# Groups of tokens side by side through the layers with a lag, and softmax scores made a second time in transposed form

## The chip, the cores and the metric

The kernel runs on one core of one Trainium2 chip. The metric is the device time of one execution in microseconds (us). A core has TensorE (PE), which multiplies matrices and writes the results to PSUM; VectorE (DVE), ScalarE (ACT) and GpSimd (POOL), which work element by element and in reductions; and SyncE (SP), which here only issues DMAs. Each engine takes its instructions from its own queue in order; they meet through semaphores. In the profile PE's matmuls and its loads of weights (PEld) have rows of their own. One float32 matmul of the program leaves two records, one transpose on PE leaves one.

## The reference

The input x is 8 sequences of 256 tokens with 128 features, in float32. Eight residual steps follow each other, each on a layer norm of x:

```
x += causal softmax attention (one head, key width 64, values through two matrices)
x += LN(t + relu(t w1 + b1) w2 + b2) * gamma + beta,   t = LN(x)      (FFN, expert 0 alone counts)
x += linear attention: (theta phi^T / sqrt(128)) g                     (no softmax)
x += the same FFN
x += retention: 16 heads, key width 8, value width 16, decaying causal mask, head norm, silu gate
x += silu(t wg) * (t wu) wd                                            (weights are int32 / 127)
x += softmax attention: 16 heads of width 8, no mask, output matrix
x += the same silu FFN
```

In the seventh step, for every head, the output row of a query is sum over keys of exp(s - m) v / sum over keys of exp(s - m), where s is the score of the query with the key and m may be any number that is the same for all keys of the query; the row's maximum keeps the exponentials in range.

## The kernel before

The 2048 tokens are cut into four groups of 512 (two sequences each). A group's x lives in SBUF as a tile of 128 partitions by 4 by 128. Every layer is a Python generator for one group: it records instructions up to a `yield`, and a driver at the end of `hybrid` decides which generator records next. A scheduling layer below takes the recorded instructions in that order as priorities, gives each tile a buffer of its pool, and may bring forward an instruction whose inputs are ready earlier; what comes out is one fixed order on each engine.

**The driver.** `parts()` lists layer by layer, and in a layer group by group. Two parts are active at a time, with the condition that they belong to different groups, and they record a step in turn. So two groups of the same layer (or the last of one layer and the first of the next) share the engines. A part that says `HEADS_NEXT` (retention and softmax attention, after their projections) waits until it is the older one of the two; its heads are copied and its values made beside the older part's heads.

**PSUM** has eight banks of 128 x 512 floats. Before: two buffers of two banks (`two_banks`), two of one bank (`one_bank`), two `held_bank`.

**Layer norm** (`layernorm`) takes statistics on DVE, the inverse root as a power on POOL, and four scalings on DVE. `transposed` turns the result on PE (L237) and copies it on ACT (L239). The first FFN (`ffn_relu`) has two layer norms, and POOL adds in between; its matmuls are L361 and L375.

**Heads.** A head has only 8 features, which would be 8 rows of the PE array. `spread_heads` (L386) copies the 16 heads' queries and keys by 16 DMAs on SP's queue (L391) so that head h lies at partitions 32 (h mod 4) to 32 (h mod 4) + 7; matmuls of heads in different groups of 32 rows may then stand in the array at once. The tile `spread` has two buffers.

**Retention** (`retention`) computes scores of 64-token chunks (L470, tiles of 8 rows by 64 columns), a state between chunks (L495, L514) and chunk values (L522, 64 by 64 tiles with 17 moving columns), and then a head norm on DVE.

**Softmax attention** (`softmax_attention`) works on pairs of heads, 16 pairs a group (2 sequences by 8). For a pair:

- `probabilities`: four score matmuls (L642; queries in rows, keys in columns) into two banks, the maxima of the rows on DVE (L648, 128 x 1024 in one instruction), and four exponentials on ACT (L654, 128 x 256 each), because each 128 queries of a head need the bias of their own maxima.
- `turned`: eight transposes of 128 x 128 on PE (L667) into held banks, and two copies of 128 x 512 on DVE (L671), so that keys lie on the partitions.
- `weighted` with `weighted_values` (L401): four matmuls with values of 32 columns a head (8 values, then ones, which give the sum of the exponentials).

After four pairs `by_query` (L406) copies the bank, turns it on PE (L414), and `divided` divides by the sums. After eight, `finished` applies the output matrix. The three steps of a pair are recorded one iteration apart: scores of pair n, transposes of pair n-1, values of pair n-2.

## Time and profile before

| | |
|---|---|
| time, median of 3 runs | 775.63 us (773.04 to 775.73) |
| the profiled execution's own time | 774.3 us |
| its span from first to last instruction | 772.2 us |
| mean granted TensorE clock | 0.829 of full |
| PE matmul busy | 653.3 us (85% of the span) |
| DVE busy | 436.2 us (56%) |
| ACT busy | 215.7 us (28%) |
| POOL busy | 108.1 us (14%) |
| table loads on ACT | 16, 1.283 us each |
| copies of heads on SP's queue | 128, 32 KB each, 0.624 us each at the median |

The stages lie one after the other: loads to 20 us, causal attention 20 to 72, first FFN 72 to 130, linear attention 130 to 156, second FFN 156 to 215, retention from 215 to about 440 with the silu FFN between 426 and 486, softmax attention 486 to 750 with the last FFN between its groups, and the end to 772.

How to read it: busy time is the time in which at least one instruction of the engine ran, so that matmuls that run side by side count once, and their mean duration says little about their pace. The pace is the distance from the start of one run of instructions to the start of the next. PEclk is the granted share of TensorE's clock. A row of a group gives its busy time and the mean length of one instruction, and then the idle time just ahead of it and what ended that.

### The profile page before, as it was taken

Reading aid. Unit: us, or ns where it says so; the run is one execution under the profiler, and the core shown is the slowest. Engines: PE = TensorE matmul, PEld = TensorE weight load, DVE = VectorE, ACT = ScalarE, POOL = GpSimd, SP = SyncE. Lnnn points to the kernel's source line nnn. Section 1 sums busy time; section 2 is a strip of 40 time slices with the busy share of each in tenths; the row PEclk is TensorE's granted clock in tenths of the full one; section 3 lists DMA queues with packets and bytes.
Section 4 is the critical chain, followed back from the end, with each engine's and each line's share of the span. In section 5 each row is a group of like instructions: output and inputs, shape, how many; then the busy total and the mean of one; then the engine's idle time right before and its main releaser. Section 6 shows DMA issues by size and latency. Waiting matters only on the chain.

```text
span 772.2 us, 12437 instructions
## 1 busy us (share of the span) xinstructions
PE 653.3 (85%) x5038; PEld 421.3 (55%) x5038; DVE 436.2 (56%) x1120; ACT 215.7 (28%) x468; POOL 108.1 (14%) x107
## 2 busy tenths in 40 slices
PE   0989574984588979989889978999999999999985
PEld 0556443662433865655556655666666666565653
DVE  3662546645583445434533455588688688766542
ACT  0333120221010011100100222544454454456541
POOL 5021233324251010110110022100000000000000
PEclk9875867995876556757655899899999999999997
DMA  7000000000003000010010000210010010000000
GB/s 227 4 1 0 1 0 1 1 0 0 1 10 45 3 1 2 12 18 2 12 18 2 2 0 1 40 16 1 1 28 2 1 28 1 1 14 1 15 14 14
DMA packets 10232, 10.49 MB, mean 14 GB/s; under 512 B 1776, under 2 KB 8512, under 8 KB 10176
## 3 DMA queue, kind: packets, MB, share of 16 engines
q1 hardware_dynamic: 9024, 9.11, 5.9%
q10 hardware_dynamic: 1152, 0.59, 0.4%
q8 instruction: 40, 0.66, 0.3%
q14 instruction: 16, 0.13, 0.1%
HBM read 4.45 MB, written 1.05 MB: 7 GB/s over the span
## 4 chain that ended last, share of the span: by engine, by line
PE 72%; DVE 15%; POOL 5%; ACT 3%; DMA 2%; issue 2%; POOLq 0%; ACTq 0%; SPq 0%; DVEq 0%
PE ps_two L642 9%; PE ps_one L401 8%; PE ps_held L667 8%; PE ps_held L522 5%; PE ps_two L361 4%; PE ps_one L495 4%; PE ps_two L470 3%; DVE ln_y L209 3%; POOL ln_rstd L217 3%; PE ps_one L607 2%; PE ps_one L237 2%; PE ps_two L598 2%; PE ps_two L437 2%; PE ps_two L599 2%; PE ps_one L375 2%; PE ps_one L567 2%
## 5 line engine op out<-in xcount | busy, mean ns | idle before, releaser
L654 ACT ACTIVATE l_p<-ps_two,l_nmax 128x256 f32<-128x256 f32 x256 | 100.5, 475 | 108.1 <-DVE l_nmax L648 108.1
L648 DVE TENSOR_REDUCE l_nmax<-ps_two 128x4 f32<-128x1024 f32 x64 | 78.3, 1223 | 41.1 <-PE ps_two L642 40.1
L217 POOL TENSOR_TENSOR ln_rstd<-ln_rstd,mhalf 128x4 f32<-128x4 f32 x40 | 40.6, 1016 | 415.8 <-DVE ln_rstd L216 415.8
L237 PE MATMUL ps_one<-ident,ln_y 128*128 128x128 f32 x128 | 31.3, 377 | 71.6 <-DVE ln_mv L205 42.3
L671 DVE COPY l_pT<-ps_held 128x512 f32<-128x512 f32 x128 | 82.6, 676 | 9.3 <-PE ps_held L667 9.2
L642 PE MATMUL ps_two<-spread 8*128 8x256 f32 x512 | 79.4, 404 | 0.3 <-DMA spread<-qk 0.3
L667 PE MATMUL ps_held<-ident,l_p 128*128 128x128 f32 x512 | 74.6, 282 | 0.8 <-ACT l_p L654 0.8
L401 PE MATMUL ps_one<-l_pT,values 128*32 128x256 f32 x512 | 73.3, 385 | 0.0
L667 PEld LDWEIGHTS ps_held<-ident,l_p 128*128 128x128 f32 x512 | 56.9, 142 | 24.0 <-ACT l_p L654 13.6
L237 PEld LDWEIGHTS ps_one<-ident,ln_y 128*128 128x128 f32 x128 | 19.9, 176 | 84.3 <-issue 54.7
L642 PEld LDWEIGHTS ps_two<-spread 8*128 8x128 f32 x512 | 48.3, 185 | 26.8 <-issue 20.3
L239 ACT COPY yT<-ps_one 128x512 f32<-128x512 f32 x32 | 18.8, 587 | 137.5 <-PE ps_one L237 137.3
L209 DVE TENSOR_SCALAR ln_y<-x,ln_mv,ln_rstd 128x128 f32<-128x128 f32 x128 | 45.2, 398 | 20.7 <-POOL ln_rstd L217 20.6
L522 PEld LDWEIGHTS ps_held<-values,r_s 64*64 64x64 f32 x1024 | 46.4, 188 | 6.0 <-issue 5.2
L522 PE MATMUL ps_held<-values,r_s 64*64 64x17 f32 x1024 | 48.0, 243 | 0.0
L252 DVE TENSOR_TENSOR x<-ps_one,x 128x256 f32<-128x256 f32 (+1 forms) x28 | 15.0, 536 | 48.2 <-PE ps_one L567 21.5
L470 PEld LDWEIGHTS ps_two<-spread 8*64 8x64 f32 x1024 | 27.9, 187 | 26.3 <-issue 19.1
L401 PEld LDWEIGHTS ps_one<-l_pT,values 128*32 128x32 f32 x512 | 27.4, 109 | 26.3 <-issue 12.7
L470 PE MATMUL ps_two<-spread 8*64 8x64 f32 x1024 | 35.6, 290 | 5.0 <-DVE r_s L475 5.0
L495 PE MATMUL ps_one<-values,r_k 64*128 64x272 f32 (+1 forms) x64 | 33.2, 640 | 4.0 <-ACT r_k L488 4.0
L204 DVE BATCH_NORM_STATS2 ln_stats<-x 128x6 f32<-128x128 f32 x128 | 31.7, 272 | 7.9 <-DMA x<-in_x 7.6
L361 PE MATMUL ps_two<-yT,c_f_w 128*128 128x512 f32 x64 | 34.4, 690 | 0.0
(144 smaller groups left out, 893.9 us busy)
## 6 DMA issues: line engine op xcount, KB each, us to landing
spread<-qk SPq DMA_DIRECT2D x128, 32.0 KB
x<-in_x SPq DMA_DIRECT2D x4, 256.0 KB
out<-x SPq DMA_DIRECT2D x4, 256.0 KB
c_f_w<-in_f_w SPq DMA_DIRECT2D x2, 256.0 KB
c_r_tab<-in_r_tab SPq DMA_DIRECT2D x1, 512.0 KB
c_r_vgb<-in_r_vgb ACTq DMA_DIRECT2D x1, 256.0 KB
c_r_qk<-in_r_qk SPq DMA_DIRECT2D x1, 256.0 KB
c_r_vg<-in_r_vg SPq DMA_DIRECT2D x1, 256.0 KB
```

What stands on the lines that cost most here:

```text
L209: nc.vector.tensor_scalar(y[:, i, :], src[:, i, :], mv[:, i, 0:1], rstd[:, i : i + 1], ALU.subtract, ALU.mult)
L237: nc.tensor.transpose(ps[:, i * P : (i + 1) * P], y[:, i, :], ident)
L361: nc.tensor.matmul(ps[:, k, :], w1[:, c * P : (c + 1) * P], yT, start=True, stop=True)
L401: nc.tensor.matmul(o[32 * i : 32 * (i + 1), (j % 2 + 1) * S - weights.shape[1] : (j % 2 + 1) * S], v, weights, start=(n == 0), stop=(n == ...
L470: nc.tensor.matmul(ps[64 * e : 64 * e + 64, k, 64 * jt : 64 * jt + 64], heads[rows, jt // 2, 1, at : at + 64], heads[rows, jt // 2, 0, at ...
L495: nc.tensor.matmul(ps[:, : HEADS * VONE], k[:rows, m, :], v[:rows, 2 * b + m, :, :VONE], start=(c == 0), stop=(c == len(pieces) - 1),)
L522: nc.tensor.matmul(ps[half, VONE * h : VONE * (h + 1)], s[half, h % 4, h // 4 * 2 + m, :], v[half, 2 * b + m, h, :VONE], start=alone, stop ...
L642: nc.tensor.matmul(ps[:, k, m * S : (m + 1) * S], qk[rows, j, 0, at + m * P : at + (m + 1) * P], qk[rows, j, 1, at : at + S], start=True, ...
L648: nc.vector.tensor_reduce(nmax, ps.rearrange("p k (m s) -> p (k m) s", m=2), AX.X, ALU.max, negate=True)
L654: nc.scalar.activation(p[:, k, m * S : (m + 1) * S], ps[:, k, m * S : (m + 1) * S], AF.Exp, bias=nmax[:, 2 * k + m : 2 * k + m + 1],)
L667: nc.tensor.transpose(ps[:, c * S + m * P : c * S + (m + 1) * P], p[:, k, m * S + c * P : m * S + (c + 1) * P], ident,)
L671: nc.vector.tensor_copy(flat(pT[:, 2 * k : 2 * k + 2, :]), ps)
```

## The change

**The driver** gives every group its own clock. Each layer has a length and a number of steps in a table; group g starts at 14 times g; at each turn the group whose clock is lowest records one step and its clock goes forward by the layer's length over its steps. So up to four groups are in different layers at once. Only one group at a time may be in retention, and only one in softmax attention; the next waits at the door.

**Buffers.** There is one spread tile for retention (`spreads[0]`) and one for softmax (`spreads[1]`), both constant tiles that POOL fills at the start: the query half with zeros, the key half with ones (four memsets of 128 x 2048). Likewise `values32[0]` belongs to retention and `values32[1]` to softmax. `one_bank` has three buffers and `held_bank` one. The hidden tile `hT` has three buffers, `probs` four, the gate of retention one; some tiles share a tag to make room. The int32 weights are made float32 in place, and `centre_values`, `prepare_ffn_int` and `prepare_lora` are recorded when group 0 comes to linear attention.

**Softmax attention.** The first scores (`scores`, L641 of the changed kernel) serve the maxima alone. The negated maxima of four pairs are gathered in one tile, turned on PE (L656), copied (L658), and four small DMAs on SP (L661) write them as a ninth row beside each head's queries; the keys have a one in that row. Six iterations later `weights` makes the scores again with keys in rows and queries in columns (L673), over 32 rows of which the ninth subtracts the maximum; the exponential (L681) then needs no bias and takes 128 x 512 at once, and its result has the keys on the partitions, as the values matmul (L691) wants. The transposes and their copies are gone. First scores of pair n and second scores of pair (n-6) with its neighbour exchanged are recorded in turn, two matmuls at a time, so that the four stand in four different row groups. The values of two pairs are recorded together, for four heads in four column groups.

```diff
-        return psum.tile([P, N], F32, tag="one", name="ps_one")
+        return psum.tile([P, N], F32, tag="one", name="ps_one", bufs=3)
-        return psum.tile([P, N], F32, tag="held", name="ps_held")
+        return psum.tile([P, N], F32, tag="held", name="ps_held", bufs=1)
...
+    spreads = []
+    for g in range(2):
+        spreads.append(const.tile([P, 4, 2, N], F32, tag=f"spread{g}", name=f"spread{g}"))
+        nc.gpsimd.memset(spreads[g][:, :, 0, :], 0.0)
+        nc.gpsimd.memset(spreads[g][:, :, 1, :], 1.0)
...
-        heads = spread_heads(qk)
-        v = values32[g % 2]
+        heads = spread_heads(qk, spreads[0])
+        v = values32[0]
...
-        qk = spread_heads(qk)
-        v = values32[g % 2]
+        qk = spread_heads(qk, spreads[1])
+        v = values32[1]
...
-        yield HEADS_NEXT
-
-        def probabilities(b, h2):
...
-            for k in range(2):
-                for m in range(2):
-                    nc.scalar.activation(
-                        p[:, k, m * S : (m + 1) * S], ps[:, k, m * S : (m + 1) * S], AF.Exp,
-                        bias=nmax[:, 2 * k + m : 2 * k + m + 1],
-                    )
+        yield
+        def place(h):
+            return slice(32 * (h % 4), 32 * (h % 4) + KDIM), h // 4
+        def scores(b, h2):
+            ps = two_banks()
+            for m in range(2):
+                for k in range(2):
+                    rows, j = place(2 * h2 + k)
+                    nc.tensor.matmul(
+                        ps[:, k, m * S : (m + 1) * S],
+                        qk[rows, j, 0, b * S + m * P : b * S + (m + 1) * P],
+                        qk[rows, j, 1, b * S : (b + 1) * S], start=True, stop=True,
+                    )
+                yield
+            h = 2 * h2 % 8
+            nc.vector.tensor_reduce(
+                nmax[b, h2 // 4][:, :, h : h + 2].rearrange("p m h -> p h m"),
+                ps.rearrange("p k (m s) -> p k m s", m=2), AX.X, ALU.max, negate=True,
+            )
+        def beside_queries(b, half):
+            ps = one_bank()
+            nc.tensor.transpose(ps[:16, :P], flat(nmax.pop((b, half))), ident)
+            rows = small.tile([16, P], F32, tag="l_rows", name="l_rows")
+            nc.vector.tensor_copy(rows, ps[:16, :P])
+            for m in range(2):
+                for j in range(2):
+                    nc.sync.dma_start(
+                        qk[KDIM : P : 32, 2 * half + j, 0, b * S + m * P : b * S + (m + 1) * P],
+                        rows[8 * m + 4 * j : 8 * m + 4 * j + 4, :],
+                    )
+        def weights(b, h2):
+            ps = [one_bank() for _ in range(2)]
+            for c in range(2):
+                for k in range(2):
+                    rows, j = place(2 * h2 + k)
+                    rows = slice(rows.start, rows.start + 32)
+                    nc.tensor.matmul(
+                        ps[k][:, c * S : (c + 1) * S],
+                        qk[rows, j, 1, b * S + c * P : b * S + (c + 1) * P],
+                        qk[rows, j, 0, b * S : (b + 1) * S], start=True, stop=True,
+                    )
+                yield
+            p = work3.tile([P, 2, N], F32, tag="probs", name="l_p", bufs=4)
+            for k in range(2):
+                nc.scalar.activation(p[:, k, :], ps[k], AF.Exp)
             return p
-        def turned(p):
...
+        def weighted(b, pairs, o):
+            for c in range(2):
+                for k in range(2):
+                    for h2, p in pairs:
+                        h = 2 * h2 + k
+                        i, j = h % 4, h // 4
+                        nc.tensor.matmul(
+                            o[32 * i : 32 * (i + 1), (j % 2) * S : (j % 2 + 1) * S],
+                            v[:, 2 * b + c, h, :], p[:, k, c * S : (c + 1) * S],
+                            start=(c == 0), stop=(c == 1),
+                        )
...
+        LAG = 6
+        nmax, made, ends = {}, [], []
+        for n in range(len(PAIRS) + LAG + 2):
+            first, second = None, None
+            if n < len(PAIRS):
+                b, h2 = PAIRS[n]
+                if h2 % 4 == 0:
+                    nmax[b, h2 // 4] = small.tile([P, 2, 8], F32, tag="l_nmax", name="l_nmax")
+                first = scores(b, h2)
+            if 0 <= n - LAG < len(PAIRS):
+                second = weights(*PAIRS[(n - LAG) ^ 1])
...
-    todo = parts()
-    upcoming = next(todo, None)
-    active = {}
-    while upcoming or active:
-        while upcoming and len(active) < 2 and upcoming[0] not in active:
...
+    layers = (
+        (causal_attention, 8.0, 12),
+        (ffn_relu, 8.0, 5),
+        (prepare, 4.0, 5),
+        (ffn_relu, 8.0, 5),
+        (retention, 20.0, 14),
+        (lambda g: ffn_silu(g, *made["ffn"]), 9.0, 5),
+        (lambda g: softmax_attention(g, made["lora"]), 28.0, 28),
+        (lambda g: last(g, *made["ffn"]), 9.0, 5),
+    )
+    LAG = 14.0
+    at = [LAG * g for g in range(GROUPS)]
+    where = [-1] * GROUPS
+    steps = [None] * GROUPS
+    while any(n < len(layers) for n in where):
+        for g in sorted(range(GROUPS), key=lambda g: at[g]):
+            if where[g] == len(layers):
+                continue
+            if steps[g] is None:
+                n = where[g] + 1
+                among_heads = n in (4, 6)
+                if n == len(layers):
+                    where[g] = n
+                    continue
+                if among_heads and any(where[o] == n and steps[o] for o in range(g)):
+                    at[g] = max(at[g], max(at[o] for o in range(g) if where[o] == n)) + 0.1
+                    continue
+                where[g], steps[g] = n, layers[n][0](g)
+            try:
+                next(steps[g])
+            except StopIteration:
+                steps[g] = None
+            at[g] += layers[where[g]][1] / layers[where[g]][2]
+            break
```

## The prediction

> **What bounds the kernel now.** I read the page's engine totals and forty slices first, then the busy time of each engine by stage, then the costliest groups, then the timeline inside softmax and inside retention, and last the waits of the DMA queue.

> ```profile
> PE 653.3 (85%) x5038; PEld 421.3 (55%) x5038; DVE 436.2 (56%) x1120; ACT 215.7 (28%) x468; POOL 108.1 (14%) x107
> PE   0989574984588979989889978999999999999985
> PEclk9875867995876556757655899899999999999997
> ```

> PE is the busiest engine, but not evenly: the first half has holes, and where retention runs (slices 13 to 22) the granted clock is low. By stage (span, then PE busy, ..., granted clock in the third column from the end):

> ```profile
> 20.00:72.00 52.00, 47.51 (x176) 29.96 (x176) 29.49 (x96) 18.43 (x52) 4.52 (x4) 0.73 0.00 1
> 72.00:130.00 58.00, 35.74 (x176) 23.89 (x174) 29.55 (x111) 7.84 (x12) 18.88 (x17) 0.79 0.00 1
> 130.00:156.00 26.00, 22.37 (x126) 14.90 (x127) 18.29 (x72) 6.39 (x13) 8.78 (x9) 0.88 0.00 1
> 156.00:215.00 59.00, 35.67 (x182) 24.05 (x180) 31.14 (x118) 7.53 (x13) 20.35 (x19) 0.80 0.00 0
> 232.00:426.00 194.00, 170.64 (x2163) 115.39 (x2161) 80.87 (x210) 20.23 (x46) 18.35 (x16) 0.61 0.07 11
> 426.00:486.00 60.00, 51.86 (x345) 34.03 (x344) 30.19 (x113) 15.04 (x28) 12.20 (x11) 0.94 0.01 2
> 750.00:772.00 22.00, 12.48 (x46) 7.29 (x46) 5.61 (x16) 4.03 (x6) 1.01 (x1) 0.82 0.04 13
> 307.00:311.00 4.00, 4.00 (x80) 4.00 (x78) 1.21 (x2) 0.77 (x3) 0.00 (x0) 0.50 0.02 4
> 495.00:525.00 30.00, 30.00 (x235) 19.28 (x235) 24.58 (x34) 15.44 (x38) 0.00 (x0) 1.00 0.13 19
> ```

> In order: causal attention, first FFN, linear attention, second FFN, retention, integer FFN, the end; then four microseconds inside retention and thirty inside softmax. The two FFN stages leave PE idle for 22.3 and 23.3 us, waiting on layernorm chains with two groups in flight. Retention leaves 23.4 us and runs at 0.61. Softmax, 486 to 750, has no hole: PE alone bounds it.

> ```profile
> L654 ACT ACTIVATE l_p<-ps_two,l_nmax 128x256 f32<-128x256 f32 x256 | 100.5, 475 | 108.1 <-DVE l_nmax L648 108.1
> L648 DVE TENSOR_REDUCE l_nmax<-ps_two 128x4 f32<-128x1024 f32 x64 | 78.3, 1223 | 41.1 <-PE ps_two L642 40.1
> L671 DVE COPY l_pT<-ps_held 128x512 f32<-128x512 f32 x128 | 82.6, 676 | 9.3 <-PE ps_held L667 9.2
> L642 PE MATMUL ps_two<-spread 8*128 8x256 f32 x512 | 79.4, 404 | 0.3 <-DMA spread<-qk 0.3
> L667 PE MATMUL ps_held<-ident,l_p 128*128 128x128 f32 x512 | 74.6, 282 | 0.8 <-ACT l_p L654 0.8
> L401 PE MATMUL ps_one<-l_pT,values 128*32 128x256 f32 x512 | 73.3, 385 | 0.0
> ```

> These are softmax's three PE groups (eight records a pair of heads each) and what ACT and DVE do beside them. Their pace is in the timeline (start, length), with one stretch at half clock (485.82), a stretch of retention, and one line of the chain, for full-array matmuls with 128 columns:

> ```profile
> 485.82 4.01 PE L642 MATMUL ps_two<-spread 8*128 8x256 f32 x16 [0.28 <-DMA spread<-qk]
> 499.04 1.09 PE L667 MATMUL ps_held<-ident,l_p 128*128 128x128 f32 x8
> 500.06 1.06 PE L401 MATMUL ps_one<-l_pT,values 128*32 128x256 f32 x8
> 501.05 1.14 PE L642 MATMUL ps_two<-spread 8*128 8x256 f32 x8
> 502.12 1.09 PE L667 MATMUL ps_held<-ident,l_p 128*128 128x128 f32 x8
> ...
> 305.67 1.16 PE L470 MATMUL ps_two<-spread 8*64 8x64 f32 x64 [0.59 <-DVE r_s L475]
> ...
> 81.31 3.59 PE ps_one L375 x32
> ```

> **The change part by part.** The profiled execution took 774.3 us (span 772.2 and 2.1 around it), 1.3 under the median of 775.63; the sum is made against 774.3.

> *Softmax on PE.* Start to start, a pair now costs 1.07 (scores) + 1.02 (transposes) + 0.99 (values) = 3.08 us, 64 pairs 197 us. The transposes go. A second set of scores of the same shape (same columns; 32 rows in place of 8) comes, placed so that it uses the two row groups which the first scores beside it leave free, and the values matmuls of two pairs stand together in four column groups. Do four small tiles run side by side? A full-array record of 128 columns takes 3.59/32 = 112 ns, so 64 columns would take 56; L470, on four tiles, gave 64 records in 1.16 us, 18 ns each: 3.1 tiles at once. Records of 256 columns would take 224 ns alone; scores now run on two row groups, 8x224/1.07 = 1.7 at once. At 3.1 the 16 records of scores and second scores in one step take 16x224/3.1 = 1.16 us, and so do the 16 of two pairs' values. In the changed kernel's order eight pairs of scores stand ahead of the first second scores (the lag in the code is six), so a group takes 8x1.07 (scores alone) + 8x1.16 (both) + 8x1.07 (second scores alone) + 8x1.16 (values) and four transposes of maxima at 0.11: 36.1 us, four groups 144: **-53 us**. Ends: only two tiles at once, 16x1.07x2 + 16x1.0 + 0.4 = 50.6 a group, 202: +5; second scores alone in fours too, 129: -68.

> *Softmax off PE.* DVE loses the 82.6 us of L671 and gains 16 copies of a 16x128 tile (nearest, the 0.25 us reciprocal of L684). The maxima are still 1.22 a pair. ACT goes from four 0.39 us exponentials a pair to two of 128x512 (nearest, the 0.59 us copy of L239). All of it lies beside PE's 1.16 + 0.58 = 1.74 a pair: nothing on the path. If that cover goes, DVE's 1.22 or ACT's 1.18 sets the pace, and both are under 1.74.
> [...]

> *Maxima and heads through SP.* Spreading a group's heads is 16 DMAs on SP, 0.67 us apart (15 took 10.04): 10.7 us. Before, two buffers let that run ahead under the group before; now softmax has one, so it waits for the last second scores of the group before. Scores can follow at two heads per 1.34 us, but the maxima's four DMAs a half stand behind all 16, and second scores behind them: 10.7 + 4x0.62 + 2.4 to land (the chain's first spread) = 15.6 us after the first issue, where six pairs last 8. Queued behind on PE are the values and everything later; two more pairs and the last FFN of the group before (8.5 us of PE) fill some. I take 8 us of idle PE for each of three groups, 24. Ends: 0, and 20 for each of four (a retention's 16 DMAs also stand between the maxima of group 0), 80.

> *Groups with a lag.* Idle PE is 772.2-653.3 = 119 us. Start: 19.2, and 2 more, as all three dequantisations now stand ahead of the first normalisation on DVE (POOL's four new memsets of 128x2048, at 1.80 each, end by 15, under the DMA that DVE awaits until 17.6). Group 0 still goes alone through four layers: of their 54 us of holes I keep half, 27. Of the 33 in 215 to 486, half, as retention now has scores and FFNs beside it: 17. End: 9.5. With softmax's 24 that is 99: **-20 us**. Ends: 60 left (-59), 150 left (+31; PE takes its instructions in order, one held bank now serves causal attention, retention and softmax, and one retention and one softmax run at a time).

> *Clock.* PE's busy time before 486 is 379 us; times the granted clock of its stages it is 276. So 103 us is the most that a full clock gives. In the rows the clock came up under 512-column full-array matmuls and fell in retention. FFN and softmax now lie among retention: I take 40%, **-41 us**; ends -103 and 0.
> [...]

> Four more table loads on ACT (16 to 20, 1.28 each) hide under PE. Sum: 774.3 - 53 - 20 - 41 = **660 us**.

> **The rivals.**
> - *Everything interleaves* (0.17): idle 75, clock -80: 774.3-53-44-80 = 597. For it: in retention, the longest stage, DVE works 81 of 194 us and ACT 20, so others fit beside it; against, the start and the end can't be filled.
> - *Two tiles only* (0.13): 660+58 = 718. For it: no row shows four row groups at work, and two give 1.7; against, the 18 ns of L470.
> - *Waits take its place* (0.13): banks, single buffers and SP leave 150 idle and the clock gains 20: 774.3-53+31-20 = 732. For it: retention's 23 idle us with two groups; against, softmax's 0.3 and 0.8 us of PE waits.
> - *The clock falls in softmax* (0.10), the slower side. The transposes, most of softmax's full-array matmuls, go; 16 score records took 4.01 us at half clock, 1.87 times 2x1.07. At half through the four softmax stages 144 us become 269: +125, and no clock gained elsewhere: 660+125+41 = 826. It decides from a loss of 114 us: with no clock gained elsewhere, from the point that six tenths of softmax's matmuls run at half. For it: retention at 0.50 with PE busy; against, values on four column groups fill the array.
> - *No gain* (0.02): the order on PE puts groups and tiles one after the other, 774.

> **How the numbers follow.** Likeliest, 0.45: 660, its own range 615 to 705. The ends don't fall together: all the good ones give 544, all the bad 810. The range 588 to 755 leaves out about 0.08 below (part of the first rival) and 0.12 above. Faster than 0.5% (about what a measurement can tell): 0.45+0.17+0.13+0.13 = 0.88; within, 0.02; slower, 0.10.

> **What would show it.** Right: no records of 128x128 transposes out of l_p; a score step and its second scores within about 1.1 us; softmax groups starting 50 to 60 us apart; PE idle near 100; causal work of the last group inside retention of the first; clock above 0.83 over the span. Wrong: 16 records of a mixed step taking 2.1 us; clock 0.50 between FFNs in the last 120 us; PE waiting long for the maxima's DMAs or for ACT's exponentials; a group period in softmax still at 65.

## The result, and the profile after

The changed kernel took 856.92 us (median of four runs, 846.46 to 866.35) against 774.34 for the kernel before on the same chip: 1.095 times as long, with a 95% interval of 1.089 to 1.101. The ratios, and every difference of times below, go by the faster of two states in which a kernel ran: for the changed kernel 846.46 and 848.46 us at a granted clock of 0.72, 847.5 at the median, where the other two runs took 865.38 and 866.35 at 0.70. I had predicted 660 us in a range of 588 to 755. The prediction was wrong in its sign.

The profiled execution took 846.46 us (span 844.7). First the page of the changed kernel: engine totals, PE and its clock in forty slices, and the groups that answer to those shown of before.

```profile
PE 712.6 (84%) x5054; PEld 420.6 (50%) x5054; DVE 361.9 (43%) x1008; ACT 190.7 (23%) x344; POOL 116.1 (14%) x111
...
PE   0757748898889988987999899989879998799985
...
PEclk9777779598959665877968696658656555575567
...
L673 PE MATMUL ps_one<-spread 32*128 32x256 f32 x512 | 117.7, 559 | 6.7 <-ACT l_p L681 6.7
L641 PE MATMUL ps_two<-spread 8*128 8x256 f32 x512 | 116.1, 546 | 7.5 <-DMA spread<-qk 2.5
...
L648 DVE TENSOR_REDUCE l_nmax<-ps_two 128x4 f32<-128x1024 f32 x64 | 78.0, 1223 | 71.9 <-PE ps_two L641 46.7
L681 ACT ACTIVATE l_p<-ps_one 128x512 f32<-128x512 f32 x128 | 70.7, 595 | 124.4 <-PE ps_one L673 116.0
```

The transposes and their copies are gone, DVE fell by 74 us. ACT, which had stood idle for 108.1 us until DVE's maxima were there, now does so for 124.4, nearly all of it until PE's scores are there; DVE waits ahead of its maxima for 71.9 us, before for 41.1. PE is still the bound and is busier than before (712.6 against 653.3 us) although it has less to do: its clock, full through softmax before, is 5 or 6 tenths in much of the second half. The same by stage, in four stretches of the span (columns: window, its length, busy PE, PEld, DVE, ACT and POOL with their counts, granted clock, DMA share, GB/s); the kernel before first, then the changed one:

```profile
0.00:140.00 140.00, 92.18 (x384) 58.88 (x385) 75.35 (x288) 29.78 (x69) 38.42 (x47) 0.79 0.11 32
140.00:300.00 160.00, 124.49 (x1003) 81.73 (x1001) 80.03 (x263) 22.09 (x40) 40.95 (x35) 0.71 0.05 8
300.00:490.00 190.00, 167.48 (x1828) 112.14 (x1827) 87.96 (x256) 30.88 (x63) 24.70 (x21) 0.73 0.05 8
490.00:772.20 282.20, 269.18 (x1828) 168.54 (x1827) 192.87 (x315) 132.94 (x298) 4.04 (x4) 0.98 0.06 11
```

```profile
0.00:140.00 140.00, 83.64 (x331) 47.78 (x332) 64.20 (x228) 24.07 (x55) 40.02 (x46) 0.82 0.11 32
140.00:300.00 160.00, 141.28 (x1452) 92.09 (x1451) 90.86 (x308) 31.78 (x63) 40.53 (x35) 0.77 0.05 8
300.00:490.00 190.00, 169.22 (x1342) 101.24 (x1340) 85.32 (x234) 44.77 (x75) 24.48 (x21) 0.73 0.06 9
490.00:844.70 354.70, 318.46 (x1938) 179.50 (x1934) 121.47 (x242) 90.12 (x151) 11.06 (x10) 0.64 0.05 9
```

From 490 on the clock is 0.64, where it had been 0.98; between 140 and 490 it was 0.77 and 0.73, before 0.71 and 0.73. Closer, in windows of 20 us inside softmax of the changed kernel, PE is busy without a gap and at half clock:

```profile
660.00:680.00 20.00, 20.00 (x129) 10.90 (x129) 7.77 (x10) 5.66 (x11) 0.00 (x0) 0.50 0.01 2
680.00:700.00 20.00, 20.00 (x109) 10.60 (x107) 6.33 (x12) 4.82 (x9) 0.00 (x0) 0.50 0.01 1
780.00:800.00 20.00, 20.00 (x109) 10.30 (x103) 7.55 (x13) 4.82 (x9) 0.00 (x0) 0.50 0.01 2
```

To put numbers on this I read PE busy time and granted clock in windows of half a microsecond and split each span into three: *work* is busy time times clock, *clock loss* is the rest of busy time, *idle* is the rest of the span. These splits are always of the profiled execution.

| us | span | PE work | clock loss | idle |
|---|---|---|---|---|
| before | 772.2 | 549.8 | 103.5 | 118.9 |
| after | 844.7 | 503.3 | 209.2 | 132.1 |
| difference | +72.5 | -46.5 | +105.7 | +13.2 |
| predicted | -114 | -53 | -41 | -20 |

So the change does on PE what it was said to do, and the clock takes back more than twice that.

### The profile page after: what moved, and what is told of

Same layout as the page of the kernel before. It is cut to its first block, busy times and chain, and to the rows that moved or that the text cites. A ratio compares the mean times of both kernels' runs of the same rounds, so it can differ in the third digit from the quotient of the medians.

```text
span 844.7 us, 12256 instructions
## 1 busy us (share of the span) xinstructions
PE 712.6 (84%) x5054; PEld 420.6 (50%) x5054; DVE 361.9 (43%) x1008; ACT 190.7 (23%) x344; POOL 116.1 (14%) x111
## 4 chain that ended last, share of the span: by engine, by line
PE 71%; DVE 11%; issue 7%; POOL 5%; ACT 3%; DMA 1%; SPq 1%; POOLq 0%; ACTq 0%; DVEq 0%
PE ps_one L673 10%; PE ps_two L641 8%; PE ps_held L691 6%; PE ps_held L519 4%; PE ps_two L595 4%; PE ps_two L596 4%; PE ps_two L369 3%; PE ps_one L604 3%; PE ps_one L492 3%; DVE ln_y L217 2%; POOL ln_rstd L225 2%; PE ps_one L245 2%; PE ps_two L467 2%; PE ps_one L383 2%; PE ps_one L411 2%
## 5 line engine op out<-in xcount | busy, mean ns | idle before, releaser
L673 PE MATMUL ps_one<-spread 32*128 32x256 f32 x512 | 117.7, 559 | 6.7 <-ACT l_p L681 6.7
L641 PE MATMUL ps_two<-spread 8*128 8x256 f32 x512 | 116.1, 546 | 7.5 <-DMA spread<-qk 2.5
L648 DVE TENSOR_REDUCE l_nmax<-ps_two 128x4 f32<-128x1024 f32 x64 | 78.0, 1223 | 71.9 <-PE ps_two L641 46.7
L681 ACT ACTIVATE l_p<-ps_one 128x512 f32<-128x512 f32 x128 | 70.7, 595 | 124.4 <-PE ps_one L673 116.0
L673 PEld LDWEIGHTS ps_one<-spread 32*128 32x128 f32 x512 | 70.4, 261 | 35.9 <-ACT l_p L681 15.9
L641 PEld LDWEIGHTS ps_two<-spread 8*128 8x128 f32 x512 | 61.2, 250 | 44.4 <-issue 21.3
L691 PE MATMUL ps_held<-l_p,values 128*32 128x256 f32 x512 | 63.6, 565 | 0.0
L595 PE MATMUL ps_two<-yT,c_g_gate 128*128 128x512 f32 x48 | 40.1, 932 | 6.8 <-DVE r_s L472 4.4
L407 DVE COPY h_oT<-ps_held 128x512 f32<-128x512 f32 x16 | 11.1, 691 | 69.7 <-PE ps_held L691 69.7
L597 ACT ACTIVATE g_hT<-ps_two 128x512 f32<-128x512 f32 x24 | 14.3, 597 | 102.2 <-PE ps_two L596 102.2
L691 PEld LDWEIGHTS ps_held<-l_p,values 128*32 128x32 f32 x512 | 19.7, 143 | 34.5 <-issue 28.4
L467 PEld LDWEIGHTS ps_two<-spread 8*64 8x64 f32 x1024 | 24.0, 177 | 23.5 <-issue 10.7
L596 PE MATMUL ps_two<-yT,c_g_up 128*128 128x512 f32 x48 | 35.5, 834 | 0.0
```

What stands on the lines that cost most here:

```text
L467: nc.tensor.matmul(ps[64 * e : 64 * e + 64, k, 64 * jt : 64 * jt + 64], heads[rows, jt // 2, 1, at : at + 64], heads[rows, jt // 2, 0, at ...
L595: nc.tensor.matmul(ps[:, 0, :], w_gate[:, cols], yT, start=True, stop=True)
L596: nc.tensor.matmul(ps[:, 1, :], w_up[:, cols], yT, start=True, stop=True)
L641: nc.tensor.matmul(ps[:, k, m * S : (m + 1) * S], qk[rows, j, 0, b * S + m * P : b * S + (m + 1) * P], qk[rows, j, 1, b * S : (b + 1) * S] ...
L648: nc.vector.tensor_reduce(nmax[b, h2 // 4][:, :, h : h + 2].rearrange("p m h -> p h m"), ps.rearrange("p k (m s) -> p k m s", m=2), AX.X, ...
L673: nc.tensor.matmul(ps[k][:, c * S : (c + 1) * S], qk[rows, j, 1, b * S + c * P : b * S + (c + 1) * P], qk[rows, j, 0, b * S : (b + 1) * S] ...
```

## The experiments

Each expectation spells out its theories with numbers. Theory 1 is that the small tiles of the new softmax, 8-row tiles above all, let the clock fall; theory 2 is the rival to it in that run. Theories 3 and 4 came up on the way and are stated where they first appear.

A 128x512 float32 matmul added to a kernel leaves two records of 0.44 us at full clock (28 such records took 12.28 us in the first bench). Several expectations below price an added matmul as one record; the true price is twice that, and the measured work shows it.

**One half of the change at a time.** `lag_old_softmax` is the changed kernel with the softmax of before (scores, biased exponentials, transposes) and its PSUM banks; `new_softmax_old_driver` is the new softmax, with the PSUM banks of after, under the driver of before, with heads ahead again.

```diff
 lag_old_softmax: the driver and layer table of after, and in softmax_attention
-        def scores(b, h2): ... def beside_queries ... def weights ... LAG = 6 ...
+        def probabilities(b, h2): ... def turned(p): ... probs, turns, ends = {}, {}, []
 new_softmax_old_driver: the softmax of after, and
-    layers = ( ... )   LAG = 14.0 ...
+    def parts(): ...   (two active parts, HEADS_NEXT)
-        qk = spread_heads(qk, spreads[1])
+        qk = spread_heads(qk, spreads[g % 2])
```

> The lag driver, one group at a time in retention and in softmax, with the softmax of before (transposes, copies, two one-bank and two held buffers). Theory 1: softmax keeps the clock near 1.00 and its 65 us a group or a little more; the mean clock of the span is above 0.80 and the time 730 to 790. Theory 2 (the driver's waits are what costs): clock below 0.75 and time over 800, near the changed kernel's 857.

> The driver of before (two groups at a time, heads of the next group copied ahead) with the new softmax (second scores, no transposes). Theory 1: from 486 us on the clock is 0.50 for most of softmax, a group takes 80 to 95 us, time 820 to 870. Theory 2: no gaps from the lag, so the clock holds, and the 53 us that left PE come off: 715 to 745.

Measured: 814.44 us (ratio 1.051, 1.047 to 1.055) and 879.62 us (1.140, 1.131 to 1.149). Neither half is a gain. Theory 1 had the clock of the first right (0.823) and its time wrong; the second came out just above theory 1's range, in its direction.

| us | span | PE work | clock loss | idle |
|---|---|---|---|---|
| lag driver, old softmax | 811.3 | 562.6 | 117.8 | 131.0 |
| old driver, new softmax | 877.8 | 496.9 | 231.3 | 149.6 |

The new softmax alone takes 53 us of work off PE, exactly the predicted term, and brings 128 us of clock loss. The lag alone costs 40 us, spread over all three columns.

**Is it the shape of the tiles?** The bench `clock_bench` runs kinds of matmul one after the other, each behind full-array matmuls; x is copied to the output and no layer is computed.

> Nothing of the reference is computed: x is copied to the output, and PE alone runs stages of dense matmuls without a wait, each behind 14 full-array 512-column matmuls (two records each) that bring the clock up: (a) four row groups with 8 rows, (b) four row groups with 32 rows, (c) four column groups of 32, (d) the changed kernel's mix of a step of scores and second scores, twice, and the values of two pairs, (e) the mix of before: scores on two row groups, eight transposes, values on two column groups, (f) transposes of 128x128, (g) ordinary matmuls of 128x128 with 128 columns. Theory 1 (small tiles side by side do not hold the clock, the transposes did): a, b and d fall to 0.50 within some 10 us and stay there, e, f and g stay at 1.00. Theory 2 (idle gaps and waits took the clock down, dense small tiles hold it): all of a to g stay at 1.00.

Its timeline (start, length, then the tile's rows by columns and the moving data) for four row groups of 8 rows and of 32 rows, and the windows (clock in the third column from the end) in those two stages:

```profile
18.79 24.37 PE L67 MATMUL bank<-x,x 8*128 8x256 f32 x256
...
56.80 14.10 PE L67 MATMUL bank<-x,x 32*128 32x256 f32 x256
```

```profile
24.00:43.00 19.00, 19.00 (x180) 15.91 (x176) 0.00 (x0) 0.00 (x0) 0.50 0.00 1
57.00:70.00 13.00, 13.00 (x244) 12.35 (x245) 0.00 (x0) 0.00 (x0) 1.00 0.01 3
```

The same 256 records behind the same full-array matmuls cost 24.4 us with 8 rows and 14.1 us with 32: within 3.6 us the 8-row tiles lost the clock (0.97 from 20.00 to 22.40 us, 0.50 from 24.00 on) and never got it back, with PE busy throughout. Column tiles, the transposes, and the changed kernel's mix (8-row and 32-row scores, values) stayed at 1.00 here: the windows 72 to 88 and 90 to 140 us read 1.00, and the mean clock of 0.954 over 258.9 us comes to 23.8 us at half, which the 8-row tiles and the 3 us behind them take up. So 8-row tiles alone dropped the clock in the bench, but the dense mix did not: shape alone does not explain the changed kernel, and neither theory is right as it stood.

**Does the clock matter at all?** `filler512` adds one 128x512 matmul, on the whole array, ahead of each pair's second scores.

```diff
             ps = [one_bank() for _ in range(2)]
+            nc.tensor.matmul(ps[0][:, : P * 4], w1[:, :P], w1[:, : P * 4], start=True, stop=True)
```

> The changed kernel with one useless full-array matmul of 128x128 by 512 columns (two records, 0.89 us at full clock) ahead of every pair's second scores, into a bank that they then overwrite: 57 us more work on PE at full clock, 114 at half. Theory 1: they hold the clock up in softmax, which falls from 97 to 65 to 75 us a group; time 760 to 815, mean clock above 0.80. Theory 2: the clock does not care, time 910 to 970.

835.07 us (1.078, 1.074 to 1.081), outside both ranges: 12 us *faster* than the changed kernel with 73 us *more* work on PE (576.7). Its clock loss fell from 209.2 to 129.7, its idle time from 132.1 to 126.6.

**Wider rows at no cost.** In `after_s32` the first scores read all 32 rows of their row group; the added rows hold zeros against ones, so results and matmul count are the same. In `after_sr32` the retention scores do so too. `newsoft_old_sr32` and `before_sr32` make both edits in the new softmax under the old driver and in the kernel before.

```diff
                     rows, j = place(2 * h2 + k)
+                    rows = slice(rows.start, rows.start + 32)
...
         qk = spread_heads(qk, spreads[1])
+        nc.sync.dma_start(qk[KDIM:P:32, :, 0, :], qk[KDIM + 1 : P : 32, :, 0, :])
```

> The changed kernel with one edit: the first scores of softmax read 32 rows of each row group instead of 8 (the rows below hold zeros against ones, and one DMA a group puts zeros back where the last group's maxima were), so the values are the same. Theory 1 (tiles of 8 rows let the clock fall, tiles of 32 rows hold it): the clock loss of 209 us falls to about 100 (retention still has tiles of 8 rows), time 725 to 775, granted clock above 0.80. Theory 2 (the gaps while steps wait for banks and DMAs let the clock fall, whatever the rows): 840 to 870, clock 0.70 to 0.73.

> As after_s32, and the scores of retention read 32 rows too (zeros against ones). Theory 1: the clock loss falls to 50 to 80, time 685 to 740, clock above 0.86. Theory 2: 840 to 870. If rows matter in softmax alone, the time of after_s32.

> The new softmax under the old driver (879.62 us with scores of 8 rows), with scores of 32 rows in softmax and retention. Theory 1: its clock loss of 231 falls to 60 to 100, time 705 to 760. Theory 2: 865 to 890.

> The kernel before with one edit: heads are spread into constant tiles whose unused rows hold zeros (queries) and ones (keys), and the scores of softmax and retention read 32 rows. Theory 1: of the clock loss of 103 the part in retention goes and that in softmax too, time 700 to 750. Theory 2: 765 to 785, as before. If theory 1 holds but transposes already held the clock in softmax, only retention gains: 735 to 765.

Measured: 798.47, 787.23, 867.26 and 774.51 us. The page of `after_s32`, to be held against L641 and the totals of the changed kernel above:

```profile
PE 657.7 (83%) x5054; PEld 392.4 (49%) x5054; DVE 361.6 (45%) x1008; ACT 189.9 (24%) x344; POOL 116.1 (15%) x111
...
L643 PE MATMUL ps_two<-spread 32*128 32x256 f32 x512 | 104.0, 497 | 9.1 <-DMA spread<-qk 4.1
```

The same number of matmuls took 55 us less of PE busy time, and 49 us came off the whole: the clock loss went from 209.2 to 148.8 with work about the same (503.3, 508.9). That is the cleanest intervention of the study. But all four miss theory 1's ranges. `after_s32` and `after_sr32` fall between the theories (725 to 775 and 685 to 740 for rows); the second gains 13 us on the first. Under the old driver the edits give 12 us (clock loss 215.4), in the kernel before nothing (ratio 0.999, 0.996 to 1.002), both inside theory 2's ranges. Rows matter; they are not the whole of it.

**Which steps drop it, and what raises it.** `clock_bench2` enters each kind of work at half clock, behind 8-row tiles, and then tries the first scores alone, with DVE's 128x1024 maximum a pair, at full clock. No layer is computed here either.

> No layers: x is copied to the output, and stages of TensorE work run one after the other. Each of the first five is entered from half clock (behind 128 records of 8 rows): the softmax mix with 32 rows of which 24 hold zeros against ones, the mix with 8 rows, dense 32-row tiles, dense 32-column tiles, transposes. Then, each entered at full clock behind 30 records of 128x512: the mix with zeros, and three forms of the first scores alone with a 128x1024 maximum on VectorE a pair (8 rows; 32 rows; 32 rows and a 128x512 record in front). Theory 1 (rows): dense 32-row tiles, column tiles and transposes bring the clock up within 7 us, the mix with 8 rows does not. Theory 3 (raising needs more than holding, and the steps alone drop it): both mixes stay at 0.50 when entered at half and the mix stays at 1.00 when entered at full; the first scores alone fall to 0.50 within 7 us with either row count, and hold 1.00 with the 128x512 record.

Windows of 3.41 us; after the engines' busy times and counts stands the clock. First the last stretch of 8-row tiles and the second stretch of the mix behind them; then the same for dense 32-row tiles; then the third stretches or later of first scores alone, with 8 rows, with 32 rows, and with 32 rows and a 128x512 matmul a pair:

```profile
81.84:85.25 3.41, 3.41 (x36) 2.23 (x35) 0.00 (x0) 0.00 (x0) 0.50 0.00 0
88.66:92.07 3.41, 3.41 (x62) 2.10 (x61) 0.00 (x0) 0.00 (x0) 1.00 0.03 5
129.58:132.99 3.41, 3.41 (x36) 2.98 (x32) 0.00 (x0) 0.00 (x0) 0.50 0.00 0
136.40:139.81 3.41, 3.41 (x70) 3.24 (x65) 0.00 (x0) 0.00 (x0) 1.00 0.02 5
361.46:364.87 3.41, 3.41 (x18) 2.38 (x18) 2.45 (x3) 0.00 (x0) 0.50 0.00 0
409.20:412.61 3.41, 3.41 (x18) 2.42 (x18) 2.45 (x2) 0.00 (x0) 0.50 0.02 5
456.94:460.35 3.41, 3.41 (x18) 1.39 (x14) 1.95 (x2) 0.00 (x0) 1.00 0.00 0
```

(In the first microseconds of a trace the clock column says 1.00 until a change is recorded; the pace there, 36 records a window, is that of half clock.) Theory 3 held for the first scores alone: two row groups of 32, half of the array, lost the clock like 8 rows did, and then did not regain it though PE was busy 3.41 of 3.41 us. It failed for the mix: entered at half, the dense mix was at full clock one stretch later, with 8 rows or 32 (62 records in 3.41 us, from 88.66 and from 37.51 us). So what the clock followed here is neither the rows of one tile nor busy time, but seems to be how much of the array is at work.

**Counting the array.** I gave every record its share of the array (tile rows times tile columns over 128 x 128) times its moving columns, at 0.442 us for 512 columns (28 such records took 12.28 us in `clock_bench`, 0.439 each), spread it evenly over the record's time, and summed this *array work* stretch by stretch on the grid on which the clock changed. All recorded changes of a trace lie on one grid of 3.413 us: in the kernel before the first and the last, at 33.82 and 771.10 us, are 216 times 3.413 us apart, and softmax's full clock lasts from 494.62 to 754.03, 76 times. How busy PE is does not tell the two clocks apart: of the windows above, all with PE busy for 3.41 of 3.41 us, four are at 0.50 and three at 1.00. Over the 18 kernels of this study that compute the layers, the kernel before among them, from the first recorded change on, what a stretch of array work (as a share of the stretch at full clock) was followed by:

| array work of a stretch | at half clock: next half / next full | at full clock: next half / next full |
|---|---|---|
| under 0.20 | 647 / 1 | 139 / 15 |
| 0.20 to 0.35 | 667 / 58 | 205 / 91 |
| 0.35 to 0.40 | 98 / 49 | 35 / 99 |
| over 0.40 | 0 / 266 | 0 / 1780 |

Over 0.40 the next stretch is at full clock in all 2046 cases. Under 0.35 a half clock stays in 1314 of 1373 cases, and a full one falls in 344 of 450: a low stretch is sometimes forgiven, by what I could not see. The table's bounds were found in some of these traces, but the six kernels that were run after they were written down agree: over 0.40 full in 766 of 766 cases, under 0.35 half stays in 375 of 390. One bound on array work (0.37) tells the next clock in 94% of all stretches; on PE's busy share no bound does in more than 70%. Counting rows alone, without the columns, reaches 93%, so these kernels hardly tell rows in use from array in use. A tile is counted by its size, zeros included (in `after_s32` 24 rows of zeros a tile took 60 us off the clock loss). And half clock halves the pace (dense 8-row tiles in `clock_bench`: 48 records in 2.40 us at 0.97, 180 in 19.00 us at 0.50), so a mix that does 0.5 at full clock does 0.25 at half, and at half, by an estimate from twice the table's 0.35 to 0.40, a mix needs 0.7 to 0.8 of the array to get out again. That is theory 4, and it fits the observations so far: transposes are tiles of 128 x 128, and softmax before did 0.53 on average in its 74 stretches, all at full clock. The changed kernel from 497 to 830 us did 0.41 in its 24 stretches at full clock and 0.29 in its 72 at half.

**Bursts and fillers by this count.** `newsoft_old_alone` and `after_alone` put a 128x512 matmul ahead of the scores in the 12 of 24 steps a group which make only first or only second scores. `newsoft_old_kick` puts six in a row at the step where the mix begins; `newsoft_old_sr32_kick` has both, with 32 rows.

```diff
 alone:
+            if alone:        # n < LAG, or n >= len(PAIRS)
+                nc.tensor.matmul(ps[:, 0, :], w1[:, :P], w1[:, : P * 4], start=True, stop=True)
 kick:
+            for i in range(6 if kick else 0):        # n == LAG
+                nc.tensor.matmul(ps[:, i % 2, :], w1[:, :P], w1[:, : P * 4], start=True, stop=True)
```

> New softmax under the old driver (879.62 us, 8 rows) with one edit: in the steps in which only first scores or only second scores are made (12 of 24 a group) a 128x512 record runs ahead of them, 48 in all for 21 us of work at full clock. Theory 3: softmax starts and ends its groups at full clock and the mix holds it: clock loss 231 to 110 to 140, time 770 to 810. Theory 1 (the 8 rows of the mix drop it): 860 to 890.

> The changed kernel (857 us) with the same edit. Theory 3: clock loss 209 to 110 to 150, time 770 to 815. Theory 1: 840 to 870.

> New softmax under the old driver, 8 rows (879.62 us), with one edit: six 128x512 records in a row where the mix of both scores begins (step 6 of each group, 24 records in all, 11 us of work at full clock). Theory 4 (the clock of a stretch of 3.41 us follows the array work of the stretch before: under about 0.37 of what the whole array could do at full clock it is half; the mix does about 0.5 at full clock and 0.27 at half, so either clock keeps itself): the records bring the clock up and the mix keeps it for its ten steps: 4 groups x about 18 us less 11: 800 to 840. If the mix can't hold the clock itself: 880 to 895.

> New softmax under the old driver with scores of 32 rows (867.26 us), a 128x512 record in each step that makes only first or only second scores, and the six records where the mix begins. Theory 4: work per stretch is over 0.37 in all steps, softmax runs at full clock: clock loss 215 to 100 to 130 for 32 us more work: 745 to 800. Otherwise: 870 to 900.

| us | time | PE work | clock loss | idle |
|---|---|---|---|---|
| newsoft_old_alone | 880.26 | 543.6 | 193.4 | 143.0 |
| after_alone | 812.65 | 548.6 | 141.7 | 121.2 |
| newsoft_old_kick | 894.63 | 518.5 | 219.6 | 146.9 |
| newsoft_old_sr32_kick | 848.37 | 571.0 | 134.9 | 138.4 |

`after_alone` is a hit: 35 us faster than the changed kernel with 45 us more work. The other three are misses: the first and the third came out where their rivals had them, the last between the two. In `newsoft_old_kick`, in the second group, the projections brought the clock up at 598 us and the burst (602.2 to 607.6) held it, but the mix behind it did only 0.29 in the stretch from 608 and lost it. I had taken 0.5 for that mix; in the kernel it stands in gaps between waits for maxima and exponentials, which the bench doesn't have. So in this kernel the 8-row mix did not hold the clock itself. With 32 rows and both fillers the clock held from 577 to 755 us without a break; but the added matmuls (74 us of work) ate most of the gain, and 19 us were left.

**The same count away from softmax.** Retention in the kernel before (232 to 426 us) is at half clock in 44 of its 55 whole stretches, at 0.21 of array work on average. `before_rfill` adds whole-array matmuls there and touches nothing else (the expectation says 68; 52 were added). `after_s32_kick_rfill` has all fillers in the changed kernel with 32 rows. `before_sr32_fill` has 32-row scores in the kernel before and fewer fillers.

```diff
 before_rfill, in retention's scores and weighted:
+                for i in range(6 if b + i2 == 0 else 1):
+                    nc.tensor.matmul(ps[:, i % 2, :], w1[:, :P], w1[:, : P * 4], start=True, stop=True)
...
                 ps = held_bank()
+                nc.tensor.matmul(ps, w1[:, :P], w1[:, : P * 4], start=True, stop=True)
 before_sr32_fill: two in place of six where i2 == 0, none elsewhere in scores, and
+                nc.tensor.matmul(ps[:, : P * 2], w1[:, :P], w1[:, : P * 2], start=True, stop=True)
```

> The kernel before, softmax untouched, with 128x512 records added to retention, where its clock is half at array work of 0.06 to 0.38: six at a group's start, one ahead of each later block of scores and of each block of weighted values (68 in all, 30 us of work at full clock). Theory 4: retention's stretches at half clock go, clock loss 103 to 45 to 70: 745 to 775 (the records eat most of the gain). If the clock does not follow the array work: 795 to 815.

> The changed kernel with first scores of 32 rows (798.47 us) and all three kinds of added records: in the steps with only one kind of scores, six where the mix begins, and in retention. Theory 4: clock loss 149 to 50 to 90 for 60 us more work, some of it in what was idle: 740 to 785. Otherwise: 820 to 860.

> The kernel before with scores of 32 rows (774.51 us) and fewer added records than before_rfill: two 128x512 matmuls ahead of each sequence's scores in retention, one 128x256 ahead of each block of weighted values (64 records, 21 us of work at full clock). Theory 4: retention is left at half clock for less of its time, clock loss 102 to 60 to 75 for 21 us: 745 to 768. If the bursts are too short to raise the clock: 780 to 795.

The clock of `after_s32_kick_rfill` in forty slices, against that of the changed kernel above:

```profile
PEclk9877789979697999988897999998997999979997
```

The clock came back nearly everywhere, with a clock loss inside the expected 50 to 90, and the kernel still took 805.89 us (1.040, 1.036 to 1.045), outside both ranges: clock loss 65.3, but PE work 625.5, 122 us more than the changed kernel. `before_rfill` has 34 us less clock loss, 17 less idle and 51 more work: 773.81 us, ratio 0.994 (0.990 to 0.998), at the slow end of theory 4's range and hardly a gain. `before_sr32_fill` took 770.94 us at the median of six runs (before 774.16), just over its range, from 752.11 to 776.40, with a granted clock between 0.858 and 0.902, more where the time was less; the runs lie too far apart for an interval. Whether that spread comes from how the program falls on the grid of stretches is not tested.

**Taking the transposes away from the kernel before.** `no_turns` leaves softmax's transposes and their copies out; the values read the exponentials as they lie, and the sums get one added in place of their reciprocal, so softmax's result isn't the reference's.

```diff
         def turned(p):
-            (eight transposes and two copies)
-            return pT
+            return p.rearrange("p k (c s) -> p (k c) s", c=2)
...
-            nc.vector.reciprocal(rsum, ps[:, :, ONES])
+            nc.vector.tensor_scalar(rsum, ps[:, :, ONES], 1.0, 1.0, ALU.add, ALU.mult)
```

> The kernel before with the transposes of softmax and their copies left out (512 records of 128x128, 74 us of PE busy time; the values read the exponentials untransposed, and the sums get one added in place of their reciprocal, so softmax's output is not the reference's). Theory 4: without them scores and values do about 0.28 us of whole-array work a pair in over 2 us, 0.12 to 0.14, so the clock falls to 0.50 through softmax, and twice the remaining 149 us is what softmax takes: 770 to 830, no gain from 74 us less work. If the clock stays at 1.00: 690 to 710.

Its page and one window inside softmax:

```profile
PE 660.2 (84%) x4526; PEld 393.3 (50%) x4526; DVE 360.0 (46%) x992; ACT 215.9 (27%) x468; POOL 108.1 (14%) x107
...
PEclk9997786986795556666656998978775695599797
```

```profile
583.00:622.00 39.00, 39.00 (x142) 19.33 (x142) 13.70 (x23) 12.12 (x32) 0.00 (x0) 0.50 0.00 0
```

789.57 us, ratio 1.022 (1.018 to 1.026): a tenth of PE's matmul records left out, 53 us of work gone, and the kernel is slower, since the clock loss rose from 103.5 to 163.4 and idle time from 118.9 to 126.4. Nothing was added on PE, and the driver, the buffers and the scores are those of before. In softmax 36 stretches were at half clock, with 0.19 of array work on average. This is the change's main effect with nothing else of the change in it.

**The lag.** `lag7_old` is `lag_old_softmax` with the lag at 7.

```diff
-    LAG = 14.0
+    LAG = 7.0
```

> The lag driver with the old softmax (814.44 us) with the lag between groups at 7 instead of 14. If the lag driver loses by group 0 running alone at the start and group 3 alone at the end: idle falls from 131 to about 115, time 785 to 805. If it loses by one group at a time in retention and softmax: 808 to 825.

800.63 us, inside the first range, but not by its reason: idle went from 131.0 to 127.5 only and the clock loss from 117.8 to 111.8. What the lag costs with the old softmax I can place, not explain: from 490 us on, PE is idle for 31.8 us and loses 35.3 to the clock, against 13.0 and 4.8 before, and work over the whole span is 13 us more.

## Why the prediction was wrong

*Softmax on PE, -53: right.* Under the old driver the new softmax has 52.9 us less work, in the changed kernel 46.5 net. Four tiles do run side by side, at about the predicted pace where the clock is full. In the timeline of the changed kernel first scores of two pairs, then second scores, 28 records in all, took from 653.37 to 655.51, 1.22 us for 16 (predicted 1.16):

```profile
653.37 1.17 PE L641 MATMUL ps_two<-spread 8*128 8x256 f32 x16
654.37 1.14 PE L673 MATMUL ps_one<-spread 32*128 32x256 f32 x12
```

Where the two kinds stand beside each other at full clock, in `newsoft_old_kick`, two of each start at 607.54, 607.86, 608.08 and 608.29.

*Clock, -41 with ends -103 and 0: this is the step that failed.* It measured +106, outside both ends. I had the right row in hand: four microseconds in retention with PE busy 4.00 of 4.00 us at 0.50, so busy time did not decide there. But I priced only a gain, by putting layers with full-array matmuls among retention, and set the loss aside in a rival. Nothing in the sum asked what had kept the clock at 1.00 through softmax. It was the transposes, "most of softmax's full-array matmuls", and the step that removed them was costed at their busy time alone. `no_turns` shows what they were worth: without them softmax has 36 stretches at 0.50, and the kernel is 15 us slower.

*The rival "the clock falls in softmax", 0.10 and 826 us, is the case.* Its mark, clock 0.50 between the FFNs of the last 120 us, is there (780 to 800 above). Its deciding point was passed: counted from the 660 us, which held a gain of 41, the clock term is 147 us worse, where 114 would do. One thing in it was off: the argument against it, that values on four column groups fill the array, holds for dense work only. In the bench the mix stayed up (1.00 from 90 to 140 us in `clock_bench`). In the kernels the steps that make only first or only second scores use at most half of the array, and the mix stands among gaps (0.29 in `newsoft_old_kick`) and at half clock did too little to raise it (the changed kernel did 0.29 on average in its 72 stretches at half); which of the two drops the clock first in the changed kernel is not shown. Its size was near: it priced 125 us for softmax at half clock, and the clock loss from 490 us on is 116.5 against 4.8. The 660, with the clock term 147 worse, idle time 33 and work 6.5, make the 846.5 of the profiled execution.

*Groups with a lag, -20: wrong in sign, by 33 us.* Idle measured +13, inside the ends (-59, +31). The parts: up to 140 us, when group 0 has left its four layers (retention's scores begin at 145), 56.4 us are idle where I had 48 (start, and half of the holes), and 47.8 before. From there on 75.7 are idle where I had 50.5 (17 in retention, 24 in softmax, 9.5 at the end): holes closed between 140 and 300 us (35.5 before, 18.7 after) but hardly between 300 and 490 (22.5, 20.8), where retention of later groups runs beside softmax, and from 490 on 36.2 stand against 13.0. The largest waits there are 6.2 us for exponentials (L681) and 5.4 for the copies behind the values (L407).

*Softmax off PE at nothing: right as far as it was tested.* ACT and DVE wait for PE (124.4 and 71.9 us of idle), not the other way round, so neither became the limit. PE was at half clock for most of softmax; what they would allow at full clock this kernel doesn't show. *Maxima and heads through SP*: PE waited 7.5 us in all ahead of the first scores and 6.7 ahead of the second, less than the 24 I took; the slow PE may hide the rest, so the term is not tested at full clock.

## What to carry to other kernels

Before removing "useless" work from the bounding engine, ask what else that work does. Here transposes, tiles of 128 x 128, kept TensorE's clock up (1.00 from 494.62 to 754.03 us with them, 0.50 in 36 stretches of softmax without), and the small tiles that replaced them were fewer microseconds of work and more of time (under the old driver 52.9 us less work and a span 105.6 us longer). Read the granted clock stage by stage, and count the share of the array that is in use in every 3.41 us: if it would fall under about 0.4, the bound found here (over it the next stretch was at full clock in 2046 of 2046 cases), price the stage at half clock as well. Where a tile can be widened with zeros for nothing, that is the cheap repair (49 us in the changed kernel, 12 and nothing in the two others); matmuls added to hold the clock mostly cost what they bring (in `before_rfill` 34 us less clock loss for 51 more of work).
